# Spreading reciprocal softmax sums over heads: one bf16 product of three parts instead of an f32 product

## The chip, the cores and the metric

One kernel runs on one NeuronCore of a Trainium2 chip. The metric is device time in microseconds (us) of one execution, as the median of several runs. The engines are named as in the profile: PE (TensorE, matrix products), PEld (its weight loads), DVE (VectorE), ACT (ScalarE), POOL (GpSimd) and SP (SyncE, which issues most DMAs). They run side by side, each through its own queue in order, and wait for one another through semaphores.

## The reference

Four layers are applied to x (16 sequences of 56 tokens, width 256), each attending to a memory of 16 x 1500 x 128. The second and the fourth layer are the same function with other weights, and they are what the change touches:

```python
q = layernorm(x, ln_q_g, ln_q_b) @ Wq * scale          # 16 heads of 64
k, v = split(media @ Wkv)                              # media: [16, 1500, 128]
sim = where(media_mask, q @ k.T, finfo.min)            # per head
attn = softmax(sim, axis=-1)
x = x + tanh(attn_gate) * ((attn @ v) @ Wo)
h = layernorm(x, ln_ff_g, ln_ff_b)
x = x + tanh(ff_gate) * (gelu(h @ W1) @ W2)
```

The first layer is a plain attention with a gate; the third has a self-attention, a cross-attention and two gated feed-forward branches. In the inputs drawn here, only positions in the last quarter of the memory are attended in layers two and four (the mask is true where a position is padding); the kernel finds that out at its start and takes a branch in which only the last 384 positions are loaded.

## The kernel before, in words

Sequences are worked in 4 groups of 4. For each layer and group there are four functions: `pre` (norms and projections before the attention), `first`, `att` (the attention itself) and `post` (output projection and feed-forward). The `post` of one group and the `pre` of the next are emitted inside the `att` of the group between, so that their dense products lie beside its attention work.

The attention of layers two and four (`att13`, L718) is cut into periods (`period`, L407). A period takes 14 blocks of 32 rows; a row is one token and one head of one sequence, so 28 tokens with 16 heads, half a sequence. Three stages overlap in one call of `period`: the period that enters gets its scores (L339 on PE: 56 small products; L350 and L354 on DVE add the mask and take maxima), the one before it gets its softmax weights (L381 on ACT, exponentials whose running sums land in `den`) and a transposition on DVE (L392), and the one before that its weighted sums over the memory (L795 on PE, three products of 128x448 in f32). The shift of the exponentials is the row maximum, brought into place by two PE transposes, L361 and L373, with L363 and L368 on DVE between them; an ACT copy at L245 hands it over, and only then do the exponentials of that period start.

The values are not projected before the weighted sum; the sums stay in the memory's 128 dimensions and are projected afterwards, by `close`. After every second sequence, so twice for each group, `close` (L723) turns 2 x 56 x 16 weighted sums in `ot` into head outputs `oT`:

1. L732: a product with the 0/1 table `m_same` adds the four partial sums of each row in `den` (32 x 56 results in PSUM).
2. L733: reciprocals on DVE, written back to `den`.
3. L737, for each of the two sequences: POOL multiplies the reciprocals with the 0/1 table `m_mine`, giving 32 x 448 values in which each row holds only its own head pair.
4. L743: an f32 product of 32 rows with `m_half` spreads these over 128 partitions; ACT (L744, recorded at L245) copies the result to `over`.
5. L751: 16 products with the value weights per half, and L757 on DVE multiplies them with `over` into `oT`.

The products of steps 1, 4 and 5, the transposes of L361 and L373 and the products of L702 (`absorbed`, which multiplies the next pair's queries with the key weights) all land in one PSUM pool, "t", with two buffers: each product waits until ACT or DVE has emptied the buffer before last. The score tiles, "sc", have three buffers. Once for each group the first pair's `close` is followed by `absorbed` for the second pair; the second pair's is followed by the dense work of `pre` and `post`, L682 (queries), L831 (output projection), L846 and L858 (feed-forward).

The order in the text of the program is not the order in the queues. A scheduler of the framework places every engine's instructions when the program is built, by its own estimates of what is ready when. So a change of a few lines can move instructions far around it.

At the start, the mask and a table of constants (`tables`, L1242, all the 0/1 tables in one transfer) are loaded. DVE looks at the mask (L1238 to L1240), a small product and L1246 decide, and every engine then takes the branch for the short or the long program.

Of the kernel before, what the change touches and what calls it, by code (L numbers as in the profile page):

```python
# [11 lines left out]
BF16 = mybir.dt.bfloat16  # L12
# [4 lines left out]
ALU = mybir.AluOpType  # L17
# [13 lines left out]
NB, BW = 12, 32  # L31
# [9 lines left out]
FFI = 1024  # L41
I2 = 688
NF2 = 6
BIG = 1.0e30
LOWEST = -3.0e38

# [16 lines left out]
def tile_kernel(ctx: ExitStack, tc: tile.TileContext, a, layers=4, groups=NG):  # L63
# [29 lines left out]
    def turn():  # L93
        return psum(ps_t, "t")
# [7 lines left out]
    def tmp(name):  # L102
        return tpool.tile([128, 512], F32, tag="tmp", name=name)
# [69 lines left out]
    def load_x(gi):  # L173
# [544 lines left out]
    def att13(name, gi, state, then, side, ends, last):  # L718
# [4 lines left out]
        def close(pr, ot, den):  # L723

            tok = slice(pr * TP, (pr + 1) * TP)
            if "oT" not in state:
                state["oT"] = big.tile([128, 8, T], F32, tag="hT", bufs=2, name="oT")
            oT = state["oT"]

            t = turn()  # L730
            total = den.rearrange("p b m -> p (b m)")
            nc.tensor.matmul(t[:BW, :N], m_same, total, start=True, stop=True)  # L732
            nc.vector.reciprocal(total[:BW], t[:BW, :N])  # L733
            over = []
            for b in range(2):
                flat = tmp("over")[:, : 8 * N]
                nc.gpsimd.tensor_tensor(  # L737
                    flat[:BW].rearrange("p (m k) -> p m k", k=H),
                    den[:BW, b].unsqueeze(2).to_broadcast([BW, N // 2, H]),
                    m_mine[:BW].unsqueeze(1).to_broadcast([BW, N // 2, H]), ALU.mult,  # L740
                )
                t = turn()
                nc.tensor.matmul(t[:, : 8 * N], m_half[:BW], flat[:BW], start=True, stop=True)  # L743
                scalar_copy(flat, t[:, : 8 * N])  # L744
                over.append(flat.rearrange("p (n j) -> p j n", j=8))
            for j0 in range(0, 8, 4):
                p = turn()
                for j in range(4):
                    for e in range(2):
                        h = 2 * (j0 + j) + e  # L750
                        nc.tensor.matmul(  # L751
                            p[e * 64 : (e + 1) * 64, j * TP : (j + 1) * TP],
                            wv[:, h * 64 : (h + 1) * 64], ot[:, :, h, :],
                            start=True, stop=True,
                        )
                for b in range(2):
                    nc.vector.tensor_tensor(  # L757
                        oT[:, j0 : j0 + 4, tok].rearrange("p j (b n) -> p b j n", b=2)[:, b],
                        p[:, : 4 * TP].rearrange("p (j b n) -> p b j n", j=4, b=2)[:, b],
                        over[b][:, j0 : j0 + 4], ALU.mult,  # L760
                    )
# [493 lines left out]
def constants():  # L1255
# [119 lines left out]
```

## Time and profile before

| what | value |
|---|---|
| median of 3 runs | 1768.75 us (1766.23, 1768.75, 1775.0) |
| profiled execution, its own time | 1774.53 us |
| span of its instructions | 1772.7 us |
| mean granted PE clock | 0.986 |
| spreading product L743 | 64 records (two for each f32 product), 534 ns in the median, 721 at most |
| sum product L732 | 32 records, 225 ns |
| reciprocal L733 | 16, 490 ns in the mean |
| POOL product L737 | 32, 965 ns in the mean |
| ACT copy to `over` | 32, 543 ns in the median |
| L757 on DVE | 64, 551 ns in the mean |

Busy times of PE are modelled and include some waiting, since products are pipelined; the distance from one record's start to the next is the better price. The granted clock is the share of full speed that PE was given; in this profile it is 1.00 or 0.50 in stretches of 3.4 us or multiples of it.

The second layer's attention lies at about 206 to 436 us of the span, the fourth's from about 1440 us to the end. The sum product runs first at 219.1 us and last at 1735.5 us.

### The profile page before, as it was taken

What the parts mean: (1) busy time and instruction counts of PE and PEld (TensorE: products, weight loads), DVE (VectorE), ACT (ScalarE), POOL (GpSimd) and SP (SyncE); (2) the same over time, 40 slices, a digit from 0 to 9 for tenths busy, and PEclk for the clock granted to TensorE, in tenths of its full rate; (3) what the DMA queues carried; (4) which work ended last, traced back from release to release, by engine and by line L of the source; (5) the groups of instructions that cost most, each with busy time, mean ns of one, the idle gap of its engine ahead of it and who ended that gap; (6) DMA issues with size and microseconds to landing.
All of it is one profiled execution on the core that took longest, in us unless ns stands there. A gap on an engine that the chain in (4) does not pass through costs nothing.

```text
span 1772.7 us, 55493 instructions
## 1 busy us (share of the span) xinstructions
PE 1668.2 (94%) x23964; PEld 1104.3 (62%) x23964; DVE 1126.1 (64%) x2742; ACT 1022.1 (58%) x3580; POOL 112.1 (6%) x238
## 2 busy tenths in 40 slices
PE   4888999999999999999999999999999999999997
PEld 2566777776664556545665556556656777777765
DVE  2344866657765666777657776576488746666672
ACT  1443976757454446553755547457555876766663
POOL 0000000000011000110000000000000000000000
PEclk9999999999999999999999999999999999999998
DMA  6431203020030121000210002211200132212120
GB/s 175 126 109 45 77 24 108 25 89 25 14 133 28 43 97 46 21 20 20 99 69 20 20 20 99 74 38 43 99 21 16 48 119 64 76 52 89 44 68 8
DMA packets 60132, 106.80 MB, mean 60 GB/s; under 512 B 7430, under 2 KB 44950, under 8 KB 59878
## 3 DMA queue, kind: packets, MB, share of 16 engines
q1 hardware_dynamic: 58726, 97.01, 17.0%
q0 software_dynamic: 1152, 6.14, 1.4%
q8 instruction: 190, 3.11, 0.7%
q14 instruction: 64, 0.52, 0.1%
HBM read 102.23 MB, written 0.92 MB: 58 GB/s over the span
## 4 chain that ended last, share of the span: by engine, by line
PE 77%; DVE 12%; ACT 6%; DMA 3%; issue 2%; POOL 1%; SPq 0%; POOLq 0%; DVEq 0%
PE sc L339 21%; PE o L795 9%; PE mm L1166 4%; ACT p L381 4%; PE o L1133 4%; DVE p L392 4%; PE mm L858 3%; PE mm L846 3%; PE mm L831 3%; PE mm L682 3%; PE mm L1179 2%; PE t L702 2%; DVE p L344 2%; PE t L1055 2%; PE t L743 2%; PE t L751 2%
## 5 line engine op out<-in xcount | busy, mean ns | idle before, releaser
L381 ACT ACTIVATE p<-p,few 128x96 f32<-128x96 f32 (+1 forms) x1344 | 588.3, 440 | 3.8
L339 PE MATMUL sc<-kt,qa 128*32 128x375 f32 x3584 | 407.8, 486 | 5.1 <-issue 3.1
L392 DVE STREAM_TRANSPOSE p<-p 128x480 f32<-128x480 f32 (+3 forms) x319 | 316.5, 1003 | 53.0 <-ACT p L381 52.1
L344 DVE CUSTOM_DVE_ANT_0 p<-sc,no_mask 128x375 f32<-128x375 f32 x448 | 236.4, 536 | 95.1 <-PE sc L339 86.3
L381 ACT ACTIVATION_READ_ACCUMULATOR p<-p,few 128x1 f32 x1344 | 252.2, 188 | 0.0
L339 PE MATMUL sc<-ktl,qa 128*32 128x96 f32 x7168 | 200.1, 249 | 2.3 <-issue 1.6
L339 PEld LDWEIGHTS sc<-kt,qa 128*32 128x32 f32 x3584 | 126.8, 109 | 107.7 <-issue 70.1
L1133 PEld LDWEIGHTS o<-p,vc 128*32 128x32 f32 x6144 | 142.9, 110 | 75.8 <-issue 51.2
L339 PEld LDWEIGHTS sc<-ktl,qa 128*32 128x32 f32 x7168 | 157.7, 110 | 34.0 <-issue 17.3
L795 PE MATMUL o<-p,kvl 128*128 128x448 f32 x384 | 167.9, 565 | 1.2 <-DVE p L392 1.2
L1133 PE MATMUL o<-p,vc 128*32 128x64 f32 (+1 forms) x6144 | 159.7, 215 | 8.7 <-DVE p L392 7.1
L245 ACT ACTIVATE few<-t 128x14 f32<-128x14 f32 (+2 forms) x128 | 22.2, 174 | 212.7 <-PE t L373 212.7
L350 DVE TENSOR_TENSOR p<-sc,mkl 128x480 f32<-128x480 f32 (+1 forms) x192 | 113.6, 607 | 25.5 <-PE sc L339 25.3
L354 DVE TENSOR_REDUCE few<-p 128x5 f32<-128x480 f32 (+1 forms) x192 | 114.4, 612 | 2.8
L795 PEld LDWEIGHTS o<-p,kvl 128*128 128x128 f32 x384 | 67.0, 191 | 55.3 <-issue 44.7
L245 ACT ACTIVATE qa<-t 128x224 f32<-128x224 f32 (+1 forms) x96 | 38.4, 420 | 91.4 <-PE t L702 62.7
L1166 PE MATMUL mm<-xT,w 128*128 128x224 f32 (+1 forms) x384 | 81.0, 360 | 1.1 <-DVE h2T L1171 0.9
L1166 PEld LDWEIGHTS mm<-xT,w 128*128 128x128 f32 (+1 forms) x384 | 65.7, 178 | 15.6 <-DVE h2T L1171 5.3
L1055 PE MATMUL t<-l2w,kt 128*32 128x128 f32 x1536 | 60.2, 275 | 6.2 <-issue 5.8
L245 ACT ACTIVATE ot<-o 128x448 f32<-128x448 f32 x64 | 33.8, 527 | 54.0 <-PE o L795 54.0
L702 PE MATMUL t<-qT,wl 64*128 64x112 f32 x512 | 55.4, 284 | 3.2 <-DVE qa L713 2.0
L757 DVE TENSOR_TENSOR oT<-t,over 128x224 f32<-128x224 f32 x64 | 31.8, 551 | 41.3 <-PE t L751 38.2
(262 smaller groups left out, 2293.8 us busy)
## 6 DMA issues: line engine op xcount, KB each, us to landing
w<-in_L_W SPq DMA_DIRECT2D x16, 1024.0 KB
kt<-in_ctxT SPq DMA_DIRECT2D x16, 768.0 KB
w<-in_L_Wq SPq DMA_DIRECT2D x8, 1024.0 KB
w<-in_L_Wo SPq DMA_DIRECT2D x8, 1024.0 KB
ktl<-in_ctxT SPq DMA_DIRECT2D x32, 192.0 KB
kvl<-in_ctx_last SPq DMA_DIRECT2D x32, 192.0 KB
w<-in_L_v_qkv SPq DMA_DIRECT2D x4, 768.0 KB
w<-in_L_l_qkv SPq DMA_DIRECT2D x4, 768.0 KB
```

The lines of the kernel that those rows point to most:

```text
L245: nc.scalar.activation(out, in_, AF.Copy, scale=scale)
L339: nc.tensor.matmul(sc[g * BW : (g + 1) * BW, at : at + w], q, k, start=True, stop=True, skip_group_check=True,)
L344: return nc.vector.tensor_tensor_reduce(u["p"][:, i, :w], sc[:, :w], u["mask"], 1.0, LOWEST, ALU.add, ALU.max, u["mx"][:, i : i + 1],).ins ...
L350: nc.vector.tensor_tensor(p, sc[:, : m * w].rearrange("p (i k) -> p i k", i=m), u["mask"].unsqueeze(1).to_broadcast([128, m, w]), ALU.add,)
L354: return nc.vector.tensor_reduce(u["mx"][:, i : i + m], p, AX.X, ALU.max).ins.name
L381: nc.scalar.activation(u["p"][:, i, : u["w"]], u["p"][:, i, : u["w"]], AF.Exp, bias=u["shift"][:, i : i + 1], accum_out=u["den"][:, i : i ...
L392: turned = nc.vector.transpose(blocks, blocks)
L702: nc.tensor.matmul(halves[e][:, j * TP : (j + 1) * TP], wkT[e * 64 : (e + 1) * 64, j0 + j, :], qT[e * 64 : (e + 1) * 64, j0 + j, tok], sta ...
L795: nc.tensor.matmul(o[:, : ub * BW], kv[:, j, :], p, start=start, stop=stop)
L1055: nc.tensor.matmul(p[g * BW : (g + 1) * BW, (j - j0) * DM : (j - j0 + 1) * DM], made["kt"][:, g, j * BW : (j + 1) * BW], cv, start=True, s ...
L1133: nc.tensor.matmul(o[cols, : pieces * BW], made["v"][:, j, cols], p.rearrange("p (i g) r -> p g i r", g=4)[:, g], start=start, stop=stop, ...
L1166: nc.tensor.matmul(p[:w, k * T : (k + 1) * T], wt[:, c, cols], xe[n][:, c, :], start=(c == 0), stop=(c == 1),)
```

## The change

Steps 1 to 4 of `close` are changed. The table `m_same` gets 96 columns instead of 32 (the same 32 three times), so the sum product gives the sums three times, on 96 partitions, and the reciprocals are taken on 96. Each reciprocal is then written as a sum of three bf16 numbers: the rounded value, the rounded rest, and the rest of that, which leaves nothing over; the first lands on partitions 64 to 95, the second on 0 to 31, the third on 32 to 63. That takes two subtractions and three copies on DVE. POOL multiplies the parts with the same 0/1 table into a bf16 tile `wide` of 96 rows, and one bf16 product with a bf16 copy of `m_half` (`half_b`, made once at the start on DVE) adds the three parts in f32 and spreads them. The weight load of the bf16 product is an instruction of its own in the program. `over` is then written by ACT as before, into a tile that POOL no longer uses.

```diff
+TH = 3 * BW
...
-        "gates": 4, "rope": 33, "m_mine": H, "m_half": 128, "m_same": BW,
+        "gates": 4, "rope": 33, "m_mine": H, "m_half": 128, "m_same": 3 * BW,
...
+    half_b = const.tile([3 * BW, 128], BF16, name="half_b")
...
             total = den.rearrange("p b m -> p (b m)")
-            nc.tensor.matmul(t[:BW, :N], m_same, total, start=True, stop=True)
-            nc.vector.reciprocal(total[:BW], t[:BW, :N])
+            nc.tensor.matmul(t[:TH, :N], m_same, total, start=True, stop=True)
+            nc.vector.reciprocal(total[:TH], t[:TH, :N])
+            parts = small.tile([128, N], BF16, tag="parts", bufs=2, name="parts")[:TH]
+            nc.vector.tensor_copy(parts, total[:TH])
+            for rest in (slice(0, 2 * BW), slice(BW, 2 * BW)):
+                nc.vector.tensor_tensor(total[rest], total[rest], parts[rest], ALU.subtract)
+                nc.vector.tensor_copy(parts[rest], total[rest])
+            parts = parts.rearrange("p (b m) -> p b m", b=2)
             over = []
             for b in range(2):
+                wide = small.tile([128, 8 * N], BF16, tag="wide", bufs=2, name="wide")[:TH]
+                nc.gpsimd.tensor_tensor(
+                    wide.rearrange("p (m k) -> p m k", k=H),
+                    parts[:, b].unsqueeze(2).to_broadcast([TH, N // 2, H]),
+                    m_mine[:TH].unsqueeze(1).to_broadcast([TH, N // 2, H]), ALU.mult,
+                )
+                t = turn()
+                nc.tensor.matmul(t[:, : 8 * N], half_b, wide, start=True, stop=True)
                 flat = tmp("over")[:, : 8 * N]
-                nc.gpsimd.tensor_tensor(
-                    flat[:BW].rearrange("p (m k) -> p m k", k=H),
-                    den[:BW, b].unsqueeze(2).to_broadcast([BW, N // 2, H]),
-                    m_mine[:BW].unsqueeze(1).to_broadcast([BW, N // 2, H]), ALU.mult,
-                )
-                t = turn()
-                nc.tensor.matmul(t[:, : 8 * N], m_half[:BW], flat[:BW], start=True, stop=True)
                 scalar_copy(flat, t[:, : 8 * N])
...
     nc.sync.dma_start(tables, a["tables"])
+    nc.vector.tensor_copy(half_b, m_half[: 3 * BW])
...
-    same = (p[:, None] % 32 == np.arange(32)).astype(np.float32)
+    same = (p[:, None] % 32 == np.arange(96) % 32).astype(np.float32)
```

More of the change, by code (lines that the diff above doesn't have):

```diff
@@ L731, in close @@
             total = den.rearrange("p b m -> p (b m)")
[L732 to L733 removed]
+            nc.tensor.matmul(t[:TH, :N], m_same, total, start=True, stop=True)
[6 more added lines that the diff above has]
+            parts = parts.rearrange("p (b m) -> p b m", b=2)
             over = []
             for b in range(2):
[L736 removed]
+                wide = small.tile([128, 8 * N], BF16, tag="wide", bufs=2, name="wide")[:TH]
                 nc.gpsimd.tensor_tensor(
[L738 to L740 removed]
+                    wide.rearrange("p (m k) -> p m k", k=H),
+                    parts[:, b].unsqueeze(2).to_broadcast([TH, N // 2, H]),
+                    m_mine[:TH].unsqueeze(1).to_broadcast([TH, N // 2, H]), ALU.mult,
                 )
                 t = turn()
[L743 removed]
+                nc.tensor.matmul(t[:, : 8 * N], half_b, wide, start=True, stop=True)
+                flat = tmp("over")[:, : 8 * N]
                 scalar_copy(flat, t[:, : 8 * N])
```

## The prediction

> **What bounds the kernel now.** I read the page first: the engines' shares, and the shares of the chain of work that ended last.
>
> ```profile
> PE 1668.2 (94%) x23964; PEld 1104.3 (62%) x23964; DVE 1126.1 (64%) x2742; ACT 1022.1 (58%) x3580; POOL 112.1 (6%) x238
> ...
> PE 77%; DVE 12%; ACT 6%; DMA 3%; issue 2%; POOL 1%; SPq 0%; POOLq 0%; DVEq 0%
> ```
>
> TensorE (PE) carries the time, but 94% is an average over stages. The change touches only `close`, which runs 16 times (2 layers x 4 groups x 2 pairs), so I next read busy times by stretch: two ordinary periods of the second layer, and the stretch around its first close.
>
> ```profile
> 231.11:236.65 5.54, 5.52 (x122) 3.72 (x121) 5.31 (x13) 2.57 (x13) 0.00 (x0) 1.00 0.01 3
> 236.65:242.18 5.53, 5.51 (x121) 3.71 (x121) 5.38 (x12) 5.50 (x31) 0.27 (x1) 1.00 0.28 79
> ...
> 218.00:231.10 13.10, 12.48 (x188) 8.79 (x186) 7.97 (x18) 10.31 (x50) 1.94 (x3) 1.00 0.10 28
> ```
>
> Columns: length, then PE, PEld, DVE, ACT, POOL busy, then granted clock. An ordinary period takes 5.5 us and PE (5.5), ACT (5.5) and DVE (5.4) are all full, so less PE work alone buys nothing there. Around a close DVE is idle for 5 us and ACT for 3 us: there a serial chain sets the pace. The timeline of that close:
>
> ```profile
> 219.38 0.50 DVE L733 RECIPROCAL den<-t 32x56 f32<-32x56 f32 x1
> ...
> 220.01 1.90 POOL L737 TENSOR_TENSOR over<-den,tables 32x448 f32<-32x448 f32 x2 [1.97 <-ACT p L381]
> ...
> 221.03 1.95 PE L743 MATMUL t<-over,tables 32*128 32x448 f32 x4 [0.40 <-POOL over L737]
> ...
> 222.91 0.37 PE L339 MATMUL sc<-ktl,qa 128*32 128x96 f32 x8
> ...
> 223.21 1.75 PE L751 MATMUL t<-ot,wl 128*64 128x112 f32 x32
> ...
> 224.31 1.95 DVE L757 TENSOR_TENSOR oT<-t,over 128x224 f32<-128x224 f32 x4 [1.95 <-PE t L751]
> ...
> 228.85 1.14 PE L702 MATMUL t<-qT,wl 64*128 64x112 f32 x8
> ...
> 234.32 0.23 PE L373 MATMUL t<-ident,nm 14*128 14x14 f32 x1
> ```
>
> The reader should see: PE waits for POOL, pays 1.9 us for two spreading products (four f32 records), then runs L751 and, through the two "t" buffers that ACT and DVE must empty, L702; only at 234.32 does L373 release ACT's next exponentials (234.80), which had had none since 229.0.
>
> **The change, part by part.** All sums are made against the profiled execution, 1774.53 us (span 1772.7, 1.8 around it). It lies 5.8 us (0.3%) above the median of the three timed runs, 1768.75; I carry the difference over to the median.
>
> *Spreading product, removed work.* The line's own rows:
>
> ```profile
> L743 PE MATMUL t<-over,tables x64: 534/534/721, 221.0 to 1740.2; 32*128 32x448 f32 x64
> ...
>   POOL over L737: 19.4, 36
> ```
>
> One close has 4 records. Two of them end to end take 0.82 us (the six records of L795, same 448 columns, take 2.45 us), so a close pays 1.64 us. In bf16 each product is one record. No bf16 product is in the trace: from above, one f32 record's spacing, 0.41 us; from below nearly nothing (0.1). I take 0.2, near the middle of these ends, since no row lies nearer. So 0.4 instead of 1.64 us, 1.24 us less PE per close, 20 us in all, if PE gets to use it.
>
> By the Trainium skill, "TensorE: Matmul & The Clock Gate", Back-to-back issue gap, an isolated warm product of 448 columns is an estimated 448/2.4 + 2.5 = 189 ns; the sum would stay within 0.4 us of itself.
>
> *Sum product and reciprocal on 96 instead of 32 rows.* L1076 does a reciprocal of 128x56 in 477 ns against 490 for L733's 32x56: rows are free. The weight load of L732 (108 ns for 32 columns) grows by at most the 191 ns row of 128 columns: 2 x 0.08 us a close, beside products; 0 to 2.5 us over 16 closes, taken as 0.
>
> *Five new DVE instructions a close* (copy, subtract, copy, subtract, copy, 56 elements a row). Nearest row: L931, 128x56, 222 ns; L1082's shortest is 206. I take 0.2, so 1.0 us a close, 16 us of DVE time in total. DVE has 5 us idle around a close, so the load is covered; if that cover were gone, it is 1 us a close. But they are a chain, and in the new order DVE puts L350 and L354 instructions of the next period between them (four of 0.58 us). POOL's product therefore starts not 0.5 us after the reciprocal but about 4.
>
> *POOL's products*, 96 rows with bf16 in and out: L1077 takes 670 ns for 128x224, L737 965 for 32x448; rows are free, elements cost. bf16 conversion shows in L147 (uint8 to bf16, 96 elements, 271 ns: no dearer per element). 0.96 us each as before; bounds 0.8 to 1.3. Behind them on POOL stands only the mask conversion L147, needed two periods later.
>
> A rule that speaks against the change: "SBUF — State Buffer", SBUF: two separate sides, says that a DVE instruction with two SBUF inputs and a GpSimd instruction shut each other out for a whole instruction. The two subtractions are such instructions. In the new order POOL has only the 0.27 us mask row near them, so the rule would add at most 0.3 us a close, 4 us in all. The trace shows no such pair (L737 ran beside transposes that kept their 0.6 us), and I add nothing.
>
> *The new order on PE.* A scheduler writes each engine's queue at build time, and it moves the spreading back. In an even close (first pair of a group) 39 score products and three L795 now stand between L373 and the spreading; in an odd close eight L682 and some score products. Walked through for the first close, on the clock of the timeline above:
> - DVE: transposes end 221.1; 5 x 0.2 + 4 x 0.58 = 3.3, last part ready 224.4. POOL: 225.4 and 226.35.
> - PE: score products to 222.1, L795 to 224.6 (before, it ran at 231.0), then idle to 225.45; spreading done 225.75 and 226.65.
> - ACT copies "over" after 13 exponentials (220.82 + 13 x 0.36 = 225.5): done 226.5 and 227.35.
> - L751: 226.55 to 228.25 (needs the "t" buffers just copied). L757: 227.5 to 229.7. L702, eight and eight: 228.7 to 231.4; the copies between no longer stand among exponentials.
> - L361 follows at once at 231.4 (before 233.40: scores and L795 came first). 36 score products, 1.7 us, stand before L373: 233.3, before 234.32.
>
> So the chain starts 4.4 us later, but 1.2 us of products and 4 us of scores and L795 are no longer in it: ACT restarts about 0.9 us earlier. Eight even closes: -7 us.
>
> In an odd close dense PE work follows, so PE's time counts directly. From the L732 of such a close, unthrottled (341.8), to the end of L751 (347.7) PE worked 5.0 of 5.9 us. New: parts ready 4.9 us after the sum product, POOL at 5.95 and 6.9; PE has 36 score products, L373 and eight L682 (1.7 + 0.2 + 3.2 us) and then waits: 1.5 us idle instead of 0.9, against 1.24 less work: -0.6 us. Seven closes: -4.
>
> The last close lies in the open tail, with no scores beside it: five DVE instructions at 0.24 add 1.2 us before POOL, the second product and copy come 0.6 us sooner after POOL, and L795 no longer hides more than before: -0.5 to +1, taken as -0.5.
>
> *Start.* The constant table grows by 64 columns (33 KB on 180) and its bf16 copy stands on DVE ahead of L1240, which releases the branch. DVE reaches that point at 4.3 us, when the table (issued at 1.65) is about in: 0 to 1 us, taken as 0.5.
>
> Sum: -7 - 4 - 0.5 + 0.5 = -11 us; 1763.5 for the profiled execution, 1757 on the median's scale.
>
> **The rivals.** *Nothing gained (about 1768).* What PE saves it spends waiting for POOL, as in the odd closes, and ACT's restart stays at 234.8 in the even ones. For it: three engines are full in ordinary periods. Against it: the walk finds 0.9 us.
>
> *Slower (about 1783).* In the even closes the late POOL product pushes L361 past its old place: the second "over" copy, at 227.35, heads everything that follows. Break-even is a chain from POOL's first result to L373 of 9 us (it was 13.3). If it only shrinks to 10.7 us, each of the eight even closes loses 1.8 us and the odd ones gain nothing: +14.
>
> *Much faster (about 1741).* PE gets all of its 20 us, and the clock helps. Granted clock around the second close:
>
> ```profile
> 250.00:254.00 4.00, 3.91 (x39) 1.88 (x37) 3.02 (x8) 3.76 (x19) 1.90 (x2) 1.00 0.19 52
> 254.00:258.00 4.00, 4.00 (x36) 3.37 (x36) 1.28 (x3) 3.55 (x19) 0.00 (x0) 0.62 0.02 6
> ```
>
> PE was busy for 3.9 of 4 us and yet ran the next 3.4 us at half clock, 1.7 us lost. In stretches of 4 us across the span, such drops follow five of the closes (254, 313, 573, 1487, 1545), each after a product with 32 of 128 rows. If 96 rows prevent them: -8.5 us, with the 20 near -28. If the new idle time brings more of them, up to ten, +17: this is the widest unknown, and I take its mean as nothing.
>
> The skill's rule on that page ("What's actually happening": a lower clock after about 3.4 us of idleness) would predict no drop here, in either kernel; the rows show drops after busy time.
>
> **How the numbers follow.** Small gain (1750 to 1762) 0.42; much faster 0.12; nothing 0.24; slower 0.22. The range 1738 to 1784 takes in the last two rivals' values. About 0.5% (8.8 us) is what a measurement of this kernel can tell from no change: faster takes 0.36 of the small gain and the 0.12, so 0.48; same 0.06 and most of nothing, 0.29; slower 0.23.
>
> **What would show it.** Bf16 records of the spreading near 0.35 us, two a close; last copy to POOL 4 to 5 us after the reciprocal; PE waiting for POOL 0.5 to 1.5 us at each close; L373 about 14.2 us after the sum product in an even close (15.3 before); ordinary periods still 5.5 us. It is wrong if the small DVE instructions take 0.4 us, if ACT's copies of "over" come later than 227.4 on that clock, or if the count of clock drops changes by more than three.

## The result and the profile after

The changed kernel takes 1773.89 us in the median of 20 runs (1765.42 to 1785.32) against 1769.55 us of the kernel before (20 runs, 1763.48 to 1775.0). The ratio is 1.0029, 95% interval 1.0015 to 1.0042: about 5 us slower, where 11 us less had been forecast. Two repeats gave 1.0031 and 1.0037 (below). The value lies inside the forecast range and within the 0.5% called "no change" there, but the direction was wrong. One run of the experiments below, 2693.82 us at a clock of 0.557 in the version with the change in the fourth layer alone, is left out of its ratio and mean clock.

The profiled execution of the changed kernel is 1774.02 us (span 1772.0, granted clock 0.985) against 1774.53 us (1772.7, 0.986): as executions the two are equal. This is its line of busy times (page of the changed kernel, busy time, share of the span, number of instructions):

```profile
PE 1650.2 (93%) x23932; PEld 1095.7 (62%) x23932; DVE 1138.1 (64%) x2823; ACT 1022.3 (58%) x3580; POOL 111.3 (6%) x238
```

PE lost 18.0 us of work (1668.2 before; 20 were predicted), and the span lost 0.7. So PE's idle time inside the span rose from 104.5 to 121.8 us. The work left as the forecast said; almost all of it came back as idleness. (The chain that ended last cannot be compared: for the changed kernel it breaks off after a tenth of the span.)

Where one sees that best is one undisturbed group of two closes, from the sum product of one first pair to the next. The columns are those of the stretches above: window and length, then PE, PEld, DVE, ACT, POOL, granted clock. First the old close, at full clock (taken from the run with one new close, described below, whose first closes are old):

```profile
220.88:309.30 88.42, 87.23 (x1238) 64.12 (x1237) 57.00 (x127) 61.81 (x271) 4.90 (x8) 1.00 0.21 68
```

Then the changed kernel, the same group:

```profile
217.93:305.80 87.87, 84.71 (x1234) 63.25 (x1233) 58.77 (x137) 61.72 (x270) 4.88 (x8) 1.00 0.22 69
```

PE's work falls by 2.5 us a group, the two times 1.24 us of the forecast, and the group by 0.55: PE's idle time rises from 1.2 to 3.2 us.

The small rows came out as predicted. These are lines of the changed kernel, per source line: duration min/median/max in ns, then first and last start and the shape. L754 is the spreading product (before L743), L748 POOL's product (L737), L742 and L743 the subtraction and the copies of the rests:

```profile
L754 PE MATMUL t<-wide,half_b x32: 349/349/421, 224.3 to 1738.9; 96*128 96x448 bf16 x32
...
  POOL wide L748: 10.3, 15
...
L748 POOL TENSOR_TENSOR wide<-parts,tables x32: 962/966/971, 223.3 to 1737.1; 96x448 bf16<-96x448 bf16 x32
...
L742 DVE TENSOR_TENSOR den<-den,parts x32: 161/206/209, 220.6 to 1735.6; 64x56 f32<-64x56 f32 x16, 32x56 f32<-32x56 f32 x16
```

One record of 349 ns a product instead of two of 534; PE waited 10.3 us for POOL in 15 closes, 0.7 each (0.5 to 1.5 predicted); POOL took 0.966 us as before, although rows and types changed; the subtractions 0.2 us.

And this is the timeline of the first close in the changed kernel, which answers the one shown of before. Line numbers have moved: L734 was L732, L352 L350, L356 L354, L341 L339, L363 L361, L370 L368, L375 L373, L704 L702, L715 L713, L763 L751, L769 L757, L247 L245. Columns: start, duration, engine, line, and in brackets the idle time before and what ended it.

```profile
217.93 0.30 PE L734 MATMUL t<-den,tables 128*96 128x56 f32 x2
...
220.01 0.14 DVE L740 CAST parts<-den 96x56 bf16<-96x56 f32 x1
220.08 0.64 DVE L352 TENSOR_TENSOR p<-sc,mkl 128x480 f32<-128x480 f32 x1
...
220.65 0.19 DVE L742 TENSOR_TENSOR den<-den,parts 64x56 f32<-64x56 f32 x1
220.76 0.64 DVE L356 TENSOR_REDUCE few<-p 128x5 f32<-128x480 f32 x1
...
223.01 0.18 DVE L743 CAST parts<-den 32x56 bf16<-32x56 f32 x1
...
223.28 1.90 POOL L748 TENSOR_TENSOR wide<-parts,tables 96x448 bf16<-96x448 bf16 x2 [6.26 <-DVE parts L743]
...
224.30 0.35 PE L754 MATMUL t<-wide,half_b 96*128 96x448 bf16 x1 [0.74 <-POOL wide L748]
...
225.50 0.68 PE L341 MATMUL sc<-ktl,qa 128*32 128x96 f32 x18
...
226.12 1.75 PE L763 MATMUL t<-ot,wl 128*64 128x112 f32 x32
...
228.38 2.04 PE L704 MATMUL t<-qT,wl 64*128 64x112 f32 x16 [0.21 <-DVE oT L769]
...
229.93 0.39 DVE L715 COPY qa<-t 128x224 f32<-128x224 f32 x1 [0.77 <-ACT qa L247]
...
230.65 1.78 PE L704 MATMUL t<-qT,wl 64*128 64x112 f32 x16
...
230.85 0.39 DVE L715 COPY qa<-t 128x224 f32<-128x224 f32 x1 [0.52 <-ACT qa L247]
...
232.68 0.28 PE L363 MATMUL t<-ident,few 128*14 128x128 f32 x1
232.81 0.66 DVE L352 TENSOR_TENSOR p<-sc,mkl 128x480 f32<-128x480 f32 x1 [0.19 <-PE sc L341]
...
233.97 0.66 DVE L352 TENSOR_TENSOR p<-sc,mkl 128x480 f32<-128x480 f32 x1
...
234.83 0.23 PE L375 MATMUL t<-ident,nm 14*128 14x14 f32 x1 [0.25 <-DVE nm L370]
```

What to see: the last part is ready 5.3 us after the sum product began because DVE puts score work (L352, L356) between the five small instructions, and PE waits for POOL at 224.30. L763 starts only at 226.12, behind 18 score products (L341). Then three of the four L715 copies are released only by an ACT copy into the same tile `qa`, so the two emptying engines work one after the other and L704 lasts until 232.4 (its last copy until 233.8); and between L363 and L375 DVE does two more L352. L375 comes 16.90 us after the sum product; before it was 15.27, and 14.2 were predicted. The waiting copies were there in the kernel before too; this is one of them, in its first close:

```profile
227.03 0.39 DVE L713 COPY qa<-t 128x224 f32<-128x224 f32 x1 [0.77 <-ACT qa L245]
```

### The profile page after: what moved, and what is told of

Read it like the earlier page. It is cut to its first block, busy times and chain, and to the rows that moved or that the text cites. A ratio compares the mean times of both kernels' runs of the same rounds, so it can differ in the third digit from the quotient of the medians.

```text
span 1772.0 us, 55499 instructions
## 1 busy us (share of the span) xinstructions
PE 1650.2 (93%) x23932; PEld 1095.7 (62%) x23932; DVE 1138.1 (64%) x2823; ACT 1022.3 (58%) x3580; POOL 111.3 (6%) x238
## 5 line engine op out<-in xcount | busy, mean ns | idle before, releaser
L341 PE MATMUL sc<-kt,qa 128*32 128x375 f32 x3584 | 408.1, 488 | 3.5 <-DVE few L346 2.7
L341 PE MATMUL sc<-ktl,qa 128*32 128x96 f32 x7168 | 201.4, 250 | 1.6 <-issue 0.6
L341 PEld LDWEIGHTS sc<-kt,qa 128*32 128x32 f32 x3584 | 126.2, 110 | 109.0 <-issue 69.3
L341 PEld LDWEIGHTS sc<-ktl,qa 128*32 128x32 f32 x7168 | 157.7, 110 | 45.2 <-issue 17.6
L247 ACT ACTIVATE few<-t 128x14 f32<-128x14 f32 (+2 forms) x128 | 22.5, 175 | 218.5 <-PE t L375 218.0
L352 DVE TENSOR_TENSOR p<-sc,mkl 128x480 f32<-128x480 f32 (+1 forms) x192 | 115.5, 609 | 32.7 <-PE sc L341 31.2
L356 DVE TENSOR_REDUCE few<-p 128x5 f32<-128x480 f32 (+1 forms) x192 | 113.8, 607 | 2.5
L247 ACT ACTIVATE qa<-t 128x224 f32<-128x224 f32 (+1 forms) x96 | 39.2, 421 | 111.2 <-PE t L704 80.8
L1067 PEld LDWEIGHTS t<-l2w,kt 128*32 128x32 f32 x1536 | 46.5, 112 | 21.7 <-issue 13.6
L704 PE MATMUL t<-qT,wl 64*128 64x112 f32 x512 | 56.6, 287 | 2.6 <-DVE oT L769 1.4
L843 PE MATMUL mm<-w,oT 128*112 128x256 f32 x256 | 58.4, 381 | 0.7 <-DVE oT L769 0.7
```

What stands on the lines that cost most here:

```text
L247: nc.scalar.activation(out, in_, AF.Copy, scale=scale)
L341: nc.tensor.matmul(sc[g * BW : (g + 1) * BW, at : at + w], q, k, start=True, stop=True, skip_group_check=True,)
L352: nc.vector.tensor_tensor(p, sc[:, : m * w].rearrange("p (i k) -> p i k", i=m), u["mask"].unsqueeze(1).to_broadcast([128, m, w]), ALU.add,)
L356: return nc.vector.tensor_reduce(u["mx"][:, i : i + m], p, AX.X, ALU.max).ins.name
L843: nc.tensor.matmul(p[:TP, i * D : (i + 1) * D], oT[:, j, i * TP : (i + 1) * TP], wo[:, j, :], start=(j == 0), stop=(j == 7),)
L1067: nc.tensor.matmul(p[g * BW : (g + 1) * BW, (j - j0) * DM : (j - j0 + 1) * DM], made["kt"][:, g, j * BW : (j + 1) * BW], cv, start=True, s ...
```

## Experiments

Closes are numbered 0 to 15; 0 to 7 lie in the second layer, 8 to 15 in the fourth; even ones follow a first pair, odd ones a second pair. "Interval" is the time from one sum product to the next. The profiles give a second number for every run, the mean granted clock. In all comparisons of this section the ratio is to the kernel before, run on the same chip in the same rounds.

### The noise: before against itself, after again

No edit.

> The kernel before, once more, for its granted clock in every run. In 20 runs of the changed kernel time fell with the clock, 1.56 us for each 0.001 (a straight line through them gives 1772.5 us at 0.986). Theory A (the changed kernel does about as well at the same clock and loses because it is granted less): the line of this kernel lies at 1773 to 1776 us at 0.986, and its mean clock is 0.987 or higher against 0.985. Theory B (the added work costs time wherever it stands): at 0.986 this kernel takes about 1768 us, 4 us less than the changed one, with the same mean clock of 0.985.

Measured: 1768.34 us, ratio 0.9995 [0.9976, 1.0014], mean clock of its runs 0.989.

> The changed kernel once more, on the same chip as the others. Ratio 1.002 to 1.004 by the measurement that stands. Theory A: the line of time over clock is the one of before or 1 to 3 us under it, with a lower mean clock. Theory B: the same mean clock, and a line 4 us above. From one sum product to the next: 32.5 us after a first pair (31.2 before), 55.4 us after a second pair in the first, second and fourth group's pattern (57.4 before).

Measured: 1772.05 us, 1.0031 [1.0016, 1.0046], mean clock 0.9855. Its profile has a span of 1764.2 us: one profiled execution says little about 5 us.

The loss is real, and it comes with a lower granted clock: in that theory A is right. Its line is not: it expected the kernel before at 1773 to 1776 us at a clock of 0.986. Over the 20 first runs of the changed kernel the time falls on a straight line against each run's own mean clock: 1.56 us more for each 0.001 less (correlation -0.93). The means are 0.985 to 0.986 in its three series, and 0.9878 to 0.9888 in six series of the kernel before. Read at the same clock of 0.986, with that slope rounded to 1.6 us, the changed kernel takes 1772.5 us (+-0.8) and the kernel before 1771.5 (+-0.6): read so, about 4 of the 5 us go with the clock, and the 1 us left is no more than its uncertainty.

### Is the late chain the loss?

Theory A: the five DVE instructions are dear because of where they stand, spread among score work, so first pairs lose and only second pairs gain. One run has the new close only where it seemed to gain, after second pairs; the old close stands in the other branch:

```diff
+            if pr == 1:
...
+            else:
...
+                nc.tensor.matmul(t[:BW, :N], m_same[:, :BW], total, start=True, stop=True)
...
```

> The change only in the close of a group's second pair, the f32 product as before in the first pair's. Theory A (the close of a first pair loses 1.35 us and that of a second pair gains 2.0): 31.2 us after first pairs and 55.4 to 56 after second ones, seven gains of 2 us, so about -14 us at the same clock: 1755 to 1759. Theory B: half of the changed kernel's loss, about +2 us: 1771 to 1772.

Measured: 1769.77 us, 1.001 [0.9988, 1.0032], mean clock 0.9839, the lowest of all versions: missed by 11 us. In its profile the undisturbed groups are 87.0 to 87.4 us, 1.2 less than with old closes, a larger gain than with both closes new (87.9). But the stretch from close 4 to close 7 took 177.1 us (167.7 before), with 27 us of it at half clock. Read at a clock of 0.986 as above, this version takes 1766.7 us (+-1.5) against 1771.5: faster, as theory A has it, but by 5 us and not by 14.

The counterpart, the new close only after first pairs, was run later (`if pr == 0:`):

> The new close only after the first pairs, the old one after the second pairs. Theory A (the late chain costs the first pairs 1.35 us each and only the second pairs gain): the eight intervals after first pairs 32.5 us against 31.2, those after second pairs 57.3 as before: 1776 to 1782 at the clock of before, ratio 1.004 to 1.008. Rival (the loss of the first pairs appears only together with the new second pairs, since the run with second pairs alone gained 1.0 and not 2.0 us on each): intervals after first pairs within 0.5 us of before's and 1768 to 1772.

Measured: 1772.01 us, 1.0019 [1.0004, 1.0034], mean clock 0.9885; the time misses theory A's 1776 to 1782 (at a clock of 0.986 it is 1775.0, +-0.9, against 1771.2 before). The intervals after first pairs are 32.6 us, as theory A has it (31.2 with old closes); those after second pairs are 56.0 although their close is the old one (57.3). So interval by interval the theory was too simple: work slides across the mark, and the group is the unit to read. By the group: old closes 88.4 to 88.6 us, first pairs new 88.6, both new 87.9, second pairs new 87.2. The first pairs cost 0.1 to 0.7, the second pairs gain 1.2.

Now the chain itself: the score instructions of the next period are held back until the last part is copied, so that the five instructions stand together; no instruction is added or left out.

```diff
+            late = line.pop("late", None)
             for i in range(0, n, u["each"]):
-                copied = scores_block(u, i)
+                with tc.issue_after(late.ins) if late else nullcontext():
+                    copied = scores_block(u, i)
...
-                nc.vector.tensor_copy(parts[rest], total[rest])
+                line["late"] = nc.vector.tensor_copy(parts[rest], total[rest])
```

> All of the change, and DVE made to finish the three copies and two subtractions before it turns to the next period's masked scores (an ordering edge without a wait). Theory A (the chain is late because four score instructions of DVE stand in it): the products of POOL start about 1.2 us after the two transposes instead of 3.2, the interval after a first pair falls from 32.5 to 30 to 31.2 us, second pairs keep 55.4: -10 to -20 us, 1750 to 1760. Theory B: no gain over the changed kernel, 1772 to 1776, since the same work is done.

Measured: 1756.48 us, 0.9932 [0.9911, 0.9953]. Theory A is confirmed where it is sharpest: the same instructions, in one piece, beat both kernels. The timeline of the first close in that run (L742, L744, L745 are the parts, L750 POOL, L756 the spreading product; the sum product began at 220.15):

```profile
222.23 0.14 DVE L742 CAST parts<-den 96x56 bf16<-96x56 f32 x1
...
222.40 0.21 DVE L744 TENSOR_TENSOR den<-den,parts 64x56 f32<-64x56 f32 x1
222.64 0.18 DVE L745 CAST parts<-den 64x56 bf16<-64x56 f32 x1
...
223.10 0.18 DVE L745 CAST parts<-den 32x56 bf16<-32x56 f32 x1
...
223.37 1.89 POOL L750 TENSOR_TENSOR wide<-parts,tables 96x448 bf16<-96x448 bf16 x2 [4.15 <-DVE parts L745]
...
224.38 0.35 PE L756 MATMUL t<-wide,half_b 96*128 96x448 bf16 x1
...
234.53 0.23 PE L375 MATMUL t<-ident,nm 14*128 14x14 f32 x1
```

The five instructions take 1.05 us instead of 3.2, the spreading starts 4.2 us after the sum product instead of 6.4 and PE does not wait for POOL before the first one, and L375 comes at 14.4 us instead of 16.9. The group, in the stretches of that run:

```profile
220.15:305.84 85.69, 84.37 (x1235) 62.54 (x1234) 58.64 (x137) 61.61 (x270) 4.87 (x8) 1.00 0.23 70
```

PE has the same work as in the changed kernel (84.4 against 84.7) and only 1.3 us of idleness instead of 3.2: the group is 2.7 us shorter than with old closes, with 2.9 us less work on PE, so nearly all that PE was spared now shows in the time. Holding back the score work was not tried on the old close. There PE idles for 1.2 us a group, so by these rows a better order alone had little to win, but no run shows it.

A repeat on another chip:

> The chain in one piece once more, for a firmer interval, on the same chip and in the same hour as the version that leaves the last group of the second layer old: 1754 to 1760, ratio 0.990 to 0.996.

Measured: 1755.75 us, 0.9928 [0.9903, 0.9953].

Is it the length of the chain rather than its place? One run takes only the first part: the sums on 32 rows, no subtractions, no rests, so the spread values have only bf16 precision.

```diff
-TH = 3 * BW
+TH = BW
...
-            for rest in (slice(0, 2 * BW), slice(BW, 2 * BW)):
-                nc.vector.tensor_tensor(total[rest], total[rest], parts[rest], ALU.subtract)
-                nc.vector.tensor_copy(parts[rest], total[rest])
...
-                nc.tensor.matmul(t[:, : 8 * N], half_b, wide, start=True, stop=True)
+                nc.tensor.matmul(t[:, : 8 * N], half_b[:TH], wide, start=True, stop=True)
```

> The bf16 product with one part alone: the reciprocals are rounded once, the two subtractions and two of the copies are left out, 32 rows, so the rests that make the result exact are missing. It prices the chain. Theory A (the length of the chain, with the score instructions inside it, is what the change loses by): interval after a first pair 29.5 to 30.5 us instead of 32.5, after a second pair 55.4 or less, and 1753 to 1759 us at 0.986. Theory B (it is the new order as such): 32 us and 1770.

Measured: 1756.95 us, 0.9944 [0.9927, 0.996], mean clock 0.989, groups of 86.6 to 87.2 us. At a clock of 0.986 that is 1762.8 us, outside the 1753 to 1759 that the theory of the length expected, and 4 us behind the chain in one piece (1758.1 and 1758.8 in its two runs; groups of 85.7). So a short chain helps too, since there is less that score work can split, but four instructions less win no more than five in one piece do.

And the bf16 product itself? One run keeps three parts but multiplies them in f32 (`wide` as an f32 tile, `m_half[:TH]` for `half_b`):

```diff
-                wide = small.tile([128, 8 * N], BF16, tag="wide", bufs=2, name="wide")[:TH]
+                wide = small.tile([128, 8 * N], F32, tag="wide", bufs=2, name="wide")[:TH]
...
-                nc.tensor.matmul(t[:, : 8 * N], half_b, wide, start=True, stop=True)
+                nc.tensor.matmul(t[:, : 8 * N], m_half[:TH], wide, start=True, stop=True)
```

> All of the change but its cheap product: the three parts go through POOL into an f32 tile and an f32 product of 96 rows. It prices the product in place. If PE gets what the product saves: 1.24 us more a close than the changed kernel, 16 to 20 us, 1788 to 1792 us at 0.986. If the product's time is hidden by waits for POOL and for ACT's copies: under 5 us more, 1772 to 1777.

Measured: 1775.26 us, 1.0042 [1.0025, 1.006], with a mean clock of 0.988. Its PE is busy for 1673.8 us, 23.6 more than in the changed kernel, but the ratios do not differ beyond their intervals. At equal clock the f32 form is 6 us slower (1778.4 against 1772.5 at 0.986), between the two expectations: the dearer product costs a quarter of what PE spends on it, as far as its own queues, which differ from the changed kernel's in places, can be left out of account.

### Where does the lower clock come from?

Theory A1: from the third layer, whose queues the scheduler rewrites although the edit does not touch it (by the profiles PE, DVE and ACT run it in another order). A2: from the new closes themselves. Layer by layer, with the condition `if name == "L1":` and then `if name == "L3":` (the second and the fourth layer):

> The change in the second layer alone, the old close in the fourth. The third layer's queues on PE and DVE then stand as in the changed kernel. Theory A1 (the lower granted clock comes with that third-layer order): half-clock windows near 599 (a double one), 722 and 1036 us as in the two profiles of the changed kernel, mean clock near 0.985, median 1771 to 1775 us. Theory A2 (the windows come at the changed closes themselves): half of the clock's loss, 0.9867, median 1769 to 1771. At a clock of 0.986 both expect 1771 to 1773.

Measured: 1774.53 us, 1.0041 [1.0019, 1.0063], mean clock 0.9856.

> The change in the fourth layer alone. The third layer's queues on PE and DVE then stand exactly as in the kernel before. Theory A1: windows in the third layer as before (573, 603, one or two of 825 and 941), mean clock 0.988, median 1766 to 1769 us. Theory A2: half of the clock's loss, 0.9867, median 1769 to 1771. At a clock of 0.986 both expect 1771 to 1773.

Measured: 1768.21 us, 1.0012 [0.9998, 1.0027], mean clock 0.9885. A loss as large as the whole comes with the second layer; what the fourth adds is not clear of zero. That fits A1, since the third layer's new order comes with it too; but it fits any cause in the second layer. So one close alone, the last of the second layer, which is enough to bring the third layer's new order:

```diff
+            if name == "L1" and gi == 3 and pr == 1:
```

> The new close in one place only, the second pair of the last group of the second layer (close 7); the fifteen other closes are as before. The scheduler then writes the third layer's PE and DVE queues exactly as in the changed kernel. Theory A1 (the lower granted clock comes with that order of the third layer): mean clock about 0.985 to 0.986, 5 us or so slower than before, 1771 to 1775, although only one close is new; half-clock windows in the third layer as in the changed kernel (5 to 6 instead of 2 to 4). Rival A2 (the lower clock comes from the new closes themselves): mean clock 0.988 as before, and a time within 2 us of before's.

Measured: 1773.01 us, 1.0022 [1.0003, 1.0041], mean clock 0.9872, against 0.9878 for the kernel before in the same rounds: the time as A1 has it, the clock not. The chain in one piece, but with old closes 6 and 7, so that the third layer keeps its order (`if not (name == "L1" and gi == 3):`):

> The version with the score instructions held back behind the last part (as in the run of the chain in one piece), but with the old close in the last group of the second layer, so that the third layer's PE and DVE queues are those of the kernel before. If chain and third-layer order are two separate causes, the gains add up: the chain in one piece was worth about 13.5 us at equal clock for 16 closes, here 14 of them, so 12 us, with a mean clock of 0.988 to 0.989: 1753 to 1757. If the third layer's order does not set the clock, the mean clock stays near the 0.987 of that run and the time is 1757 to 1760.

Measured: 1760.91 us, 0.995 [0.9933, 0.9968], mean clock 0.9858. A miss: with the old order of the third layer the clock is not higher but lower, and the time is longer than with 16 new closes. The two halves apart once more, beside the changed kernel itself; theory B is A1 without the clock, C says that every close costs its share. First the changed kernel with old closes 6 and 7 (`if not (name == "L1" and gi == 3):`):

> The changed kernel with the old close in the last group of the second layer (closes 6 and 7), so that 14 of 16 closes are new and the third layer's PE and DVE queues are those of the kernel before. The timed slowdown of the changed kernel is 5 us; with the last close alone new it was 4 us. Theory B (the slowdown is the third layer's, through its order): no slowdown here, ratio 0.996 to 1.000, 1761 to 1768. Rival C (it comes from the closes wherever they are, about a third of a us each): ratio 1.002 to 1.004, 1771 to 1775.

Measured: 1776.13 us, 1.0045 [1.0023, 1.0066], mean clock 0.9847. Theory B expected no slowdown: as the whole cause it falls, and A1 with it.

> The changed kernel once more, on the same chip in the same rounds, so that the two others are compared with it directly: 1771 to 1775, ratio 1.002 to 1.004, mean clock 0.985. A third profile of it, read for half-clock time in the third layer: 13 to 21 us by theory B, against 7 to 14 us where the third layer's queues are those of before.

Measured: 1772.59 us, 1.0037 [1.0017, 1.0056], mean clock 0.9859; 17.1 us of half clock in the third layer.

> The new close in one place only (second pair of the second layer's last group), once more, since the first interval, 1.0003 to 1.0041, is wide. Theory B: ratio 1.001 to 1.003 again. Rival C: one close in sixteen costs nothing that shows, ratio 0.999 to 1.0005.

Measured: 1770.14 us, 1.0011 [0.9996, 1.0027], mean clock 0.9883. Between the two: this one close and the third layer's order may cost 2 to 3 us together (the two intervals reach up to 5 and 7). In the profiles, nine with the new order have a third layer (close 7 to close 8) of 884.2 us in the mean, nine with the old order 882.4, and single ones scatter by 2 us (the f32 product and the single part, with a third order, are not counted): that part stays unsettled.

What is left are closes 0 to 5. Theory D: any new close of the second layer lowers the clock. Theory E: it is the stretch in which the third group's closes meet the dense work that ends the layer. First `if name == "L1" and gi < 2:`, then `if name == "L1" and gi == 2:`.

> The new close only in the first two groups of the second layer (closes 0 to 3, clean groups without dense work of another layer behind them); all else, the third layer's queues too, as before. By the profiles a clean group is 0.5 us shorter with the new close, so at the clock of before 1 us faster. Theory D (the lower clock belongs to the second layer's first closes, wherever): mean clock 0.986 or less, ratio 1.001 to 1.003. Theory E (it belongs to the stretch where the third group's closes meet the dense work that ends the layer): mean clock 0.988 to 0.989, ratio 0.998 to 1.000.

Measured: 1770.52 us, 1.0009 [0.999, 1.0027], mean clock 0.9878 (before in the same rounds: 0.9878).

> The new close only in the third group of the second layer (closes 4 and 5), all else, the third layer's queues too, as before. The profiles of the changed kernel have close 4 to close 6 1.2 us longer. Theory E: mean clock 0.986 or less, ratio 1.001 to 1.004, with 10 to 14 us of half clock between close 4 and close 7 (3 to 10 where the old close stands there). Theory D: 0.987 to 0.988, ratio within 0.001 of 1.0005.

Measured: 1775.64 us, 1.0037 [1.0021, 1.0054], mean clock 0.9866. Two new closes of sixteen, 4 and 5, make a loss as large as all sixteen do, with the third layer's old order, while the four before them cost nothing that shows. In time theory E holds. In the clock it does not: 0.9866 lies above its 0.986, and read at a clock of 0.986 this version takes 1777.2 us (+-1.4) against 1771.7 (+-0.6) of the kernel before in the same rounds. So most of this loss does not go with the mean clock, whereas most of the changed kernel's does. Nor do the parts add up: the versions with closes 0 to 3, 4 and 5, 7, and 8 to 15 new lose 0.0009, 0.0037, 0.0011 and 0.0012, together 0.007 where all sixteen lose 0.003, though each of these is uncertain by 0.0015 or more. The stretches of that run, close 4 to close 6 and close 6 to close 7, and then one of its half-clock windows with what stands ahead of it:

```profile
396.24:504.00 107.76, 98.56 (x1341) 64.38 (x1339) 76.12 (x178) 60.55 (x278) 4.60 (x7) 0.90 0.08 23
504.00:575.94 71.94, 68.51 (x637) 42.51 (x636) 36.62 (x93) 36.58 (x135) 8.97 (x16) 0.98 0.26 89
474.60:481.40 6.80, 5.30 (x138) 4.12 (x137) 5.46 (x14) 2.60 (x9) 0.00 (x0) 1.00 0.11 32
481.40:488.40 7.00, 7.00 (x50) 4.59 (x49) 3.78 (x10) 5.73 (x30) 0.00 (x0) 0.51 0.01 2
```

The same two stretches in the run with closes 0 to 3 new and closes 4 to 7 old, with its one half-clock place there:

```profile
394.73:494.60 99.87, 92.60 (x1352) 59.52 (x1351) 74.21 (x169) 60.62 (x278) 4.62 (x7) 0.97 0.09 25
494.60:562.37 67.77, 65.81 (x629) 41.02 (x628) 36.95 (x92) 36.55 (x134) 8.93 (x16) 1.00 0.28 94
479.40:486.20 6.80, 4.73 (x117) 3.30 (x116) 6.31 (x18) 3.58 (x13) 0.00 (x0) 1.00 0.36 119
486.20:493.20 7.00, 6.42 (x24) 2.52 (x26) 3.85 (x10) 5.42 (x28) 0.00 (x0) 0.51 0.00 1
```

Read the third number from the end, the granted clock: 0.90 against 0.97, then 0.98 against 1.00. The contrast is larger than usual: the first profile is the slowest of that version's twelve runs (1784.24 us), the second one of the fast ones (1764.89 us against a median of 1770.52). All profiles with the spread-out chain or none in closes 4 and 5, as length of the stretch from close 4 to close 7 and half-clock time in it:

| closes 4 and 5 | length, us | half clock, us |
|---|---|---|
| old: before, before again, fourth layer only, last close (two runs), first four closes | 167.7, 168.8, 167.6, 166.3, 168.7, 167.6: mean 167.8 | 6.8, 10.2, 6.8, 3.4, 10.2, 6.8: mean 7.4 |
| new: after (three runs), second layer only, all but the last group, third group only | 170.1, 171.3, 172.0, 174.9, 176.0, 179.7: mean 174.0 | 6.8, 10.2, 10.2, 17.1, 17.1, 23.9: mean 14.2 |

If half clock costs half its length (an estimate), 3.4 of the 6.2 us between the means are clock and 2.8 are the new order of the queues at full clock. Reckoned so, the lengths at full clock do not overlap (163.6 to 164.5 us old, 166.2 to 167.8 new); the half-clock times do. Two profiles stand outside the table because only one of the two closes is new: with close 4 (first pairs) 165.1 us with 3.4 of half clock, with close 5 (second pairs) 177.1 with 27.3. At full clock both would be 163.4 to 163.5, no longer than with old closes; so far as one profile each can tell, it takes both closes to lengthen the stretch, and close 5 alone can bring the half clock.

Does that stretch also hold back the version in one piece? It was run with old closes 4 to 7 (`if not (name == "L1" and gi >= 2):`, with the scores held back as above):

> The chain in one piece (score instructions held back behind the last part), with the old close in the third and fourth group of the second layer (closes 4 to 7), so 12 of 16 closes are new and the third layer's queues are those of before. If the loss sits in the stretch from close 4 to close 7: in the runs with the chain in one piece this stretch took 170.6 to 172.8 us against 167.8 in the mean with old closes there, so 3 us less here than in those runs; the clean groups gain 2.7 us each as there (five of them), the last group and the tail 3.5: about 17 us less than before, 1750 to 1755, ratio 0.989 to 0.993, mean clock 0.988 to 0.990. If the loss does not sit there: 1756 to 1760.

Measured: 1755.61 us, 0.994 [0.9921, 0.9959], mean clock 0.9876; in its profile the stretch is 168.2 us (170.6 and 170.7 with 16 new closes) and the span 1751.8. The median is no better than with 16 closes (0.9932 and 0.9928), so the expected 3 us do not show.

## Why the prediction was wrong

**Right.** The work taken from PE (18 us on the page against 20; 2.5 a group), the price of the small DVE instructions (0.14 to 0.21 us against 0.2), POOL's unchanged price, the start (the copy of L1255 took 0.22 us at 4.4 us; the first sum product ran at 217.9 us against 219.1), and the walk through the first close up to the second copy of `over`: it ended 8.2 us after the sum product; 8.3 were predicted.

**The failed step** lies behind that copy, and the larger part of it is "L702, eight and eight: 228.7 to 231.4; the copies between no longer stand among exponentials". The copies no longer stand among exponentials, but they are serial: DVE copies waited for ACT copies, so the two eights took 4.05 us instead of 2.7 (4.5 before). That wait could be read in the kernel before, where DVE waited 17.6 us for ACT ahead of these copies, in 22 waits (18.1 in 23 now); it did not go away with the exponentials. Ahead of this step "L751: 226.55 to 228.25" began 0.7 us too late, 8.2 us after the sum product instead of 7.5, since 18 score products stood before it on PE. And "36 score products, 1.7 us, stand before L373" left DVE out: two L352 stood there, 2.15 us instead of 1.9. Of the 2.65 us by which L375 came later than forecast, 0.8 were lost before L704, 1.35 in it and 0.5 behind it. So POOL's first result to L375 took 10.6 us (224.25 to 234.83). The forecast itself had put the break-even at 9 and priced 10.7 as the rival "slower": +1.8 us for each even close. Measured on the interval after a first pair: +1.35. Of the signs that the forecast named, only the time of L373 shows the failure; its three signs of being wrong did not come (the small instructions took 0.2 us, the second copy of `over` ended at 227.3 on the forecast's clock, and the profiles have 13 drops of the clock before and 10 after).

**The odd closes** gained 2.0 us on their interval instead of 0.6, but 1.3 of that also appears where only first pairs are new: it is work that slid across the mark. The sum by the group is what counts, -0.55 us measured against the -1.5 forecast (-0.9 and -0.6). Over eight groups that would be -4.4 instead of -11. The rival "nothing gained", that PE spends what it saves waiting, is what the page shows: 18.0 us less work, 17.3 more idleness. The gain that the forecast sought was there to be had: with the five instructions in one piece the kernel is 12 us faster, and L375 comes at 14.4 us in its first close, 14.2 having been forecast.

**Closes left out of the walk.** Two clean intervals were carried over to all sixteen. Between close 4 and close 7 the dense work that ends the layer lies between the closes, and there the stretch became 2.8 us longer at full clock; from close 14 to 15 it was 1.4 longer (23.4 against 22.1).

**The clock** was named the widest unknown and its mean taken as nothing. It was not nothing: 0.003 less, which goes with about 4 of the 5 us. The idea that half-clock drops follow the 32-row product and that 96 rows prevent them failed: the runs spent more time at half clock with 96 rows, not less. Nor did the drops that it started from hold: in a second profile of the kernel before, drops follow three closes within 6 us instead of five, and only one of them the same close.

So the sum, from the profiles: undisturbed groups -2.2 (four), close 12 to 14 -0.4, close 14 to 15 +1.4, tail about 0, close 4 to 7 +3.3 (171.1 us in the three profiles of the changed kernel against 167.8), third layer +1.8 with an uncertainty as large: +3.9, where the timed runs say +5 (2.7 to 7.4). With all six profiles with new closes 4 and 5, three of them of other versions, close 4 to 7 counts +6.2 and the sum is +6.8.

**Shown and open.** Shown: the place of the five instructions costs the gain (same instructions in one piece, with the score work held back: -12 us, twice), and closes 4 and 5 alone bring a loss of the size of the whole. Open: where the lower clock comes from. Between closes 4 and 7 there is more half clock with closes 4 and 5 new (14.2 us against 7.4 in the mean of six profiles of each kind, with ranges that overlap), but the changed kernel's own three profiles have only 9.1 there, and no run changed only one thing just ahead of a window. Open too is whether the losses of the parts add up.

## What to carry to other kernels

A few small instructions on an engine that is nearly full cost what stands between them, not their own time: hold the other work back until a chain that others wait for is through. Walk such a change to the point where the chain ends, on every engine that empties a shared buffer, and do it also for a place where the neighbours differ. When the engine that carries the time gets less work and the span stays, look at its idle time group by group, and read at least some runs' clocks before a difference of 0.3% is put down to instructions.

## What the runs showed of the hardware

- One program's time differs from run to run with the granted clock: 1.6 us for 0.001 of its mean over 1770 us. The lost time comes in pieces of 3.41 us or multiples of it at half clock, 40 to 62 us in most profiles (34 in two), and their places differ between profiles of the same kernel.
- These windows follow stretches in which PE was mostly busy (5.30 of 6.80 us, 4.73 of 6.80, above), not an idle stretch. The Trainium skill, "TensorE: Matmul & The Clock Gate", What's actually happening, lets the clock drop after a window of about 3.4 us without work; the length agrees, the condition is not what these rows show. Leaving out the first 60 us and the last 15, the 20 profiles have 177 such windows. In the 6.8 us ahead of them no pause of PE reached 3.4 us, and in 54 of them none reached 1 us (by busy times, which are modelled). The page's section "A second HAM failure mode: psum-queue depth-cycling" describes drops through many small pauses between groups of products. The 1.5 to 2.1 us of pauses in the 6.80 us ahead of the windows above would fit that; the drops of before after 3.9 busy us of 4 would not, and no run here tested it.
- A product of 96 x 448 takes one record of 349 ns in bf16 and two records of 591 ns in f32, in the median; with 32 rows the two f32 records were 534 ns each. POOL's product over 448 elements took 0.966 us whether f32 or bf16, 32 or 96 rows.
